# Four tiles for each buffer of gathered rows, and their four TensorE transposes placed at four points of a step

## The chip, the cores and the metric

The kernel runs on one core of one Trainium2 chip. The metric is device time in microseconds (us), from the start to the end of one execution. Names used here: TensorE (PE in the profile; PEld is its weight load, PEq and PEldq its sequencer), VectorE (DVE), ScalarE (ACT), GpSimd (POOL), and SyncE (SP), which only issues DMAs here. PSUM is the memory that TensorE writes, in banks of 128 x 512 float32.

## The reference

A graph of 12,500 nodes with 16 features and 412,500 directed edges, sorted by destination, goes through two blocks; each is followed by a residual and a normalisation over the 16 features. The first is a two-layer graph convolution. The second is a mesh network with two message-passing rounds, and it holds the change:

```
n = ln(mlp(x));  e = ln(mlp(edge_attr))                      # 64 features each
for s in range(2):
    ce  = concat([e, n[src], n[dst]])                        # one row of 192 per edge
    e   = e + ln(silu(ce @ w0[s] + b0[s]) @ w1[s] + b1[s])
    agg = segment_sum(e, dst)
    n   = n + ln(mlp(concat([n, agg])))
out = mlp(n)
```

`n[src]` is a gather of 412,500 rows at random places. `n[dst]` and the sum over `dst` are local, since the edges are sorted by destination.

## The kernel before

**Groups and steps.** Edges are taken in 405 groups of 1024: K = 8 columns of 128 edges, a column to a set of 128 partitions. `edge_step(s)` (L997) handles round s. Its `steps()` (L1048) is one long unrolled program: step g starts some stages of new groups and ends others of older groups, so that several groups are in flight. In round 0, step g computes the hidden layer of the edge encoder of group g (`hidden_enc`, L963), its second layer one step later, the block's hidden layer of group g - 3 (`hidden_blk`, L970), the block's second layer of group g - 4 and the segment sum of group g - 5. In round 1 there is no encoder, and the three block stages are 0, 1 and 2 steps behind. The call `tc.manual_schedule` (L1129) keeps TensorE, VectorE and ScalarE in exactly the order in which the program is written. SyncE and GpSimd are queues of their own, each in its own order, and they run ahead as far as their waits let them.

**The gathered rows.** The product of w0 with the sender's features is made once per node and stored in a table of [12500, 64] float32 in DRAM. `ahead(g)` (L1028) calls `gather` (L404), which issues eight indirect DMAs from GpSimd: each fetches 128 rows of 256 bytes into column k of a buffer `pg` of [128, 8, 64]. There are R = 5 such buffers in a ring, and `ahead` is called LA = 3 groups ahead. GpSimd does nothing else in these stages, and what holds it back is only that buffer g % 5 must have been read by the group five before. These waits are kept by pieces of the buffer: GpSimd's DMAs of columns 0, 2, 4 and 6 wait for one TensorE instruction each, the transposition of the pair of columns that they begin to overwrite.

**The block's hidden layer.** `hidden_blk` fills one PSUM bank. It multiplies w0's part for the edge features with `e` (float32, L974), adds the receiver's part by three bfloat16 products `qd` x `ot` (also L974; `qd` is a window of the receivers' table, `ot` a one-hot matrix), and then adds the gathered rows by four transposes against the identity (L976), one for each pair of columns. ScalarE reads the bank (SiLU, L979) into `h`, which the second layer (`second`, L984 for the bias and L986 for the products) takes in the next step.

**The order on TensorE in a step of round 0:** second layers of encoder and block (2 x L984, L986), transposes of normalised rows (`turned`, L994), segment sum (`window_sum`, L389, 8 columns x 2 operands), encoder's hidden layer (L965), then `hidden_blk`: `e` (L974), `qd` (L974), four transposes of `pg` (L976). Round 1 is the same without the encoder's parts and without L994. ScalarE's `h` (L979) ends every step, and the next step's second layer of the block begins with it. VectorE adds the segment sum of the step before at L397, builds `ot` at L1045 and the one-hot matrix of the sum at L377, and normalises (L466 to L471).

Of the kernel before, what the change touches and what calls it, by code (L numbers as in the profile page):

```python
# [9 lines left out]
F32 = mybir.dt.float32  # L10
# [8 lines left out]
P = 128  # L19
K = 8  # L20
W = 64
D = 64
GB = 135
SI, DR = 81, 45
R, LA = 5, 3
# [12 lines left out]
def gcn_then_mesh_gnn_kernel(ctx: ExitStack, tc: tile.TileContext, a: dict, out: bass.AP):  # L38
# [21 lines left out]
    nc = tc.nc  # L60
# [64 lines left out]
    def bank(name):  # L125
        return psum.tile([128, 512], F32, name=f"ps_{name}")
# [251 lines left out]
                                drl[:, g * K:(g + 1) * K, None].to_broadcast([P, K, W]), op=OP.is_equal)  # L378
        return oh

    def window_sum(oh, offs, g, val, acc, r0, m, later=None):


        ps = bank("seg")
        for k in range(K):
            r = r0
            for v in val(k):
                n = v.shape[1]
                nc.tensor.matmul(ps[r:r + n, :W], v, oh[:, k, :], start=(k == 0), stop=(k == K - 1))  # L389
                r += n  # L390

        def add():
            at = nc.values_load(offs[0:1, g:g + 1], engines=[ET.DVE], min_val=0, max_val=N,
                                skip_runtime_bounds_check_because="a destination is a node's number or N, and "
                                "the windows behind it are held to N")
            w = acc[r0:r0 + m, ds(at, W)]
            nc.vector.tensor_add(w, w, ps[r0:r0 + m, :W])  # L397

        if later is None:
            add()  # L400
        else:
            later.append(add)

    def gather(table, idx, to):  # L404

        for k in range(K):
            nc.gpsimd.indirect_dma_start(  # L407
                out=to[:, k, :], out_offset=None, in_=table,
                in_offset=bass.IndirectOffsetOnAxis(ap=idx[:, k:k + 1], axis=0))

    def trip_count(i, most):
        return nc.values_load(trips[0:1, i:i + 1], min_val=0, max_val=most,
# [554 lines left out]
        nc.scalar.activation(h, ph, AF.Silu, bias=ee_b0)  # L967
        return h

    def hidden_blk(s, e, pg, more=()):  # L970

        ph = bank("h")
        for i, (w, v) in enumerate([(eb_w0[s], e), *more]):
            nc.tensor.matmul(ph, w, v, start=(i == 0), stop=False)  # L974
        for j in range(KP):
            nc.tensor.matmul(ph[:, j * P:(j + 1) * P], pg[:, 2 * j:2 * j + 2, :].rearrange("p k f -> p (k f)"),  # L976
                             ident, start=False, stop=(j == KP - 1), is_transpose=True)
        h = work.tile([128, KP * P], F32, name="h")
        nc.scalar.activation(h, ph, AF.Silu, bias=eb_b0[s])  # L979
        return h  # L980

    def second(h, w1, b1):
        po = bank("o")
# [13 lines left out]
    def edge_step(s):  # L997


        ring = [work.tile([P, K, D], F32, name=f"pg{i}", bufs=1) for i in range(R)]  # L1000
        acc = (s01, 0, 128) if s == 0 else (ns2, D, D)

        ENC, ENC2, TURN, BLK, BLK2, SUM = (0, 1, 2, 3, 4, 5) if s == 0 else (None, None, None, 0, 1, 2)
# [23 lines left out]

        def ahead(g):  # L1028
            at = g % SI * K
            gather(tabs_p[s], srcs[g // SI][:, at:at + K], ring[g % R])  # L1030

        def send_window(g):
            at = nc.values_load(base_row[0:1, g:g + 1], engines=[ET.SP], min_val=0, max_val=N,
# [14 lines left out]
        def steps():  # L1048
            for g in range(2):
                send(g)  # L1050
                send_window(g)
            hot(0)
            later = []
            for g in range(NG + SUM + 1 + CHUNK):
                if real(g + 2):
                    send(g + 2)
                if g + 8 - SUM >= 0 and real(g + 8 - SUM) and (g + 8 - SUM) % DR == 0:
                    send_places((g + 8 - SUM) // DR)
                if real(g - BLK + LA) and g >= BLK:
                    if (g - BLK + LA + 8) % SI == 0 and real(g - BLK + LA + 8):  # L1060
                        send_sources((g - BLK + LA + 8) // SI)
                    ahead(g - BLK + LA)
                if real(g - BLK + 2) and g - BLK >= 0:
                    send_window(g - BLK + 2)

                while later:
                    later.pop(0)()

                if real(g - SUM + 1):
                    c = g - SUM + 1  # L1070
                    ohs[c] = one_hot(work, drls[c // DR], c % DR)
                if real(g - BLK + 1) and g - BLK >= 0:
                    hot(g - BLK + 1)

                parts = []
                if s == 0 and real(g - ENC2):
                    c = g - ENC2
                    y0[c] = work.tile([P, K, D], F32, name="y0", bufs=5)
                    parts.append((second(hids.pop(c), *ee1), y0[c]))
                if real(g - BLK2):  # L1080
                    c = g - BLK2
                    y1[c] = work.tile([P, K, D], F32, name="y")
                    parts.append((second(hidb.pop(c), *eb1[s]), y1[c]))
                if g - 1 in chunk_at:
                    c = chunk_at[g - 1]
                    ny[c] = work.tile([P, CB, D], F32, name="ny", bufs=1)
                    parts.append((node_second(nh, *nb1[s], n=P, name="seg"), ny[c]))
                if parts:
                    normalised(work, P, *parts)
                if s == 0 and real(g - TURN):  # L1090
                    c = g - TURN
                    es[c] = work.tile([128, KP * P], F32, name="e", bufs=6)
                    nc.scalar.activation(es[c], turned(y0[c]), AF.Identity, scale=e_g[0])
                if real(g - SUM):
                    c = g - SUM
                    y, e = [y1.pop(c)], es.pop(c)
                    if s == 0:
                        later.append(lambda c=c, e=e, pt=turned(y[0]): (
                            nc.vector.scalar_tensor_tensor(e, pt, e_g[1], e, op0=OP.mult, op1=OP.add),
                            nc.sync.dma_start(e1_d[:, col(c)], e)))  # L1100
                        y.insert(0, y0.pop(c))
                    window_sum(ohs.pop(c), base_row, c, lambda k: [v[:, k, :] for v in y], *acc, later)
                if s == 0 and real(g):
                    hids[g] = hidden_enc(feats.pop(g))
                if real(g - BLK):
                    c = g - BLK
                    hidb[c] = hidden_blk(s, es[c], ring[c % R], hots.pop(c))

                if g in chunk_at:
                    node_hidden(step_products(s, chunk_at[g]), nb_b0[s], nh)  # L1110
                if g - 2 in chunk_at:
                    c = chunk_at[g - 2]
                    step_update(s, c, node_turned(ny.pop(c)))
                if g - 3 in chunk_at:
                    c = chunk_at[g - 3]
                    if s == 0:
                        send_tables(1, c)
                    else:
                        dh[c] = decode_hidden(c)
                if s and g - 4 in chunk_at:  # L1120
                    c = chunk_at[g - 4]
                    decode_second(c, dh.pop(c))
# [113 lines left out]
```

## Time and profile before

The median is 16592.26 us, of 14 runs from 16435.23 to 18125.43 us. The profiled execution took 16677.06 us; its span from the first to the last instruction is 16675.1 us, and the mean clock granted to TensorE is 0.799 of the full one.

| stretch | from, us | length, us | steps |
|---|---|---|---|
| before round 0 (sort, convolution, tables) | 0 | 5466 | |
| round 0, steps with gathers | 5466.42 | 6210.30 | 400 |
| round 0, last steps, no gathers left | 11676.72 | 27.56 | 4 |
| between the rounds, start of round 1 | 11704.28 | 125.88 | |
| round 1, steps with gathers | 11830.16 | 4759.55 | 398 |
| round 1, last steps, no gathers left | 16589.71 | 22.30 | 4 |
| end | 16612.01 | 63 | |

Steps are counted from one ScalarE `h` (L979) to the next.

How lines are read. A line of waits gives the engine, the line that waited, what released it, the total in us, the number of times and the longest. "remote" means that the instruction began when a semaphore came in, and that the work which the trace names for it had ended well before. A line of the timeline gives start, length, engine, line, operation, tiles, and in brackets how long the engine had been idle and what ended that. A line of windows gives from:to, the length, then for each engine its busy us and its number of instructions, the granted clock of TensorE as a share, the DMA engines' share, and GB/s. The ends of matmuls are modelled, so their starts are used. SPq lines are DMAs that SyncE issues.

### The profile page before, as it was taken

To read this page: it belongs to the slowest core of one execution; us is meant where nothing else is said; L and a number is where in the kernel's file an instruction comes from. 1 tells how busy PE (TensorE), PEld (TensorE's weight loads), DVE (VectorE), ACT (ScalarE), POOL (GpSimd) and SP (SyncE) were. 2 spreads that over 40 slices of the span, in tenths; PEclk is the share of its full clock that TensorE was granted. 3 is DMA by queue.
4 is the path that set the end of the run, shared out by engine and by line. 5 is a ranking of instruction groups with operands and counts; after the bars stand their busy time and mean duration, and the time that the engine had idled before them with its cause. 6 is when DMAs were issued, how large, how long until landed. Compare 5 with 4: busy or idle time off the path is not lost. (4 is left out here: it accounts for less than half of the span.)

```text
span 16675.1 us, 273242 instructions
## 1 busy us (share of the span) xinstructions
PE 11848.1 (71%) x103832; PEld 8743.1 (52%) x104442; DVE 8838.4 (53%) x22535; ACT 2342.7 (14%) x3705; POOL 6211.7 (37%) x6598
## 2 busy tenths in 40 slices
PE   0096999899995777777777777777556666666665
PEld 0086999699993444444444444444344444444443
DVE  9976777577774444444444444444333433443434
ACT  3300000000001122222222222222111111111111
POOL 0000000000000554444544445444566666666665
PEclk9998999799995777777777777777777777777777
DMA  0002111111111222222222222222222222222222
GB/s 26 4 11 57 67 66 66 44 68 66 66 59 33 48 54 52 51 50 50 53 49 53 47 50 52 49 48 51 58 60 61 60 61 61 60 61 60 60 60 49
DMA packets 1009226, 873.88 MB, mean 52 GB/s; under 512 B 650006, under 2 KB 757370, under 8 KB 1007214
## 3 DMA queue, kind: packets, MB, share of 16 engines
q1 hardware_dynamic: 800512, 643.03, 13.3%
q0 software_dynamic: 207360, 212.75, 7.5%
q8 instruction: 855, 14.01, 0.3%
q14 instruction: 499, 4.09, 0.1%
HBM read 720.51 MB, written 134.51 MB: 51 GB/s over the span
## 5 line engine op out<-in xcount | busy, mean ns | idle before, releaser
L407 POOL DMA_INDIRECT pg<-tab_p,si x6480 | 6206.5, 958 | 9558.6 <-DMA qd<-tab_q 4585.0
L466 DVE TENSOR_REDUCE var<-sq 128x8 f32<-128x512 f32 (+2 forms) x1290 | 861.8, 669 | 3306.9 <-ACT sq L465 1791.5
L986 PE MATMUL ps_o<-eb_w,h 128*128 128x128 f32 x6480 | 1303.5, 363 | 1691.3 <-ACT h L979 1413.8
L598 PE MATMUL ps_h<-t,roh 128*128 128x112 bf16 (+1 forms) x39936 | 2132.0, 211 | 237.0 <-DVE roh L574 237.0
L389 PE MATMUL ps_seg<-oh,y 128*64 128x64 f32 x19440 | 1505.1, 256 | 937.0 <-issue 910.8
L598 PEld LDWEIGHTS <-roh 128*128 128x128 bf16 x39936 | 2011.0, 98 | 286.6 <-DVE roh L574 240.7
L986 PEld LDWEIGHTS ps_o<-eb_w,h 128*128 128x128 f32 x6480 | 1106.4, 258 | 1931.8 <-ACT h L979 1527.2
L389 PEld LDWEIGHTS ps_seg<-oh,y 128*64 128x64 f32 x19440 | 1240.5, 166 | 1099.5 <-issue 1072.0
L614 PE MATMUL ps_seg<-ohd,msg 128*112 128x112 f32 (+1 forms) x13312 | 1619.6, 266 | 0.0
L974 PE MATMUL ps_h<-e,eb_w 128*128 128x512 f32 x1620 | 1391.3, 945 | 130.0 <-issue 99.4
L614 PEld LDWEIGHTS ps_seg<-ohd,msg 128*112 128x112 f32 (+1 forms) x13312 | 1408.6, 173 | 0.5
L605 DVE TENSOR_TENSOR msg<-ps_h,wm 128x448 f32<-128x448 f32 (+1 forms) x1536 | 973.9, 634 | 459.9 <-PE ps_h L598 454.6
L602 DVE TENSOR_TENSOR ohd<-ior,rdrel 128x448 f32<-128x448 f32 (+1 forms) x1536 | 1009.9, 658 | 236.6 <-PE ps_seg L614 236.6
L465 ACT ACTIVATE sq<-ps_o 128x512 f32<-128x512 f32 (+1 forms) x1240 | 735.5, 593 | 2623.0 <-issue 910.4
L979 ACT ACTIVATE h<-ps_h,eb_b 128x512 f32<-128x512 f32 x810 | 556.1, 686 | 3625.2 <-remote 2382.2
L965 PE MATMUL ps_h<-at,ee_w 16*128 16x512 f32 x810 | 685.2, 909 | 327.2 <-issue 310.0
L974 PE MATMUL ps_h<-ot,qd 128*128 128x512 bf16 x1821 | 718.1, 491 | 194.8 <-issue 179.5
L974 PEld LDWEIGHTS <-qd 128*128 128x128 bf16 x2430 | 304.9, 126 | 1048.5 <-issue 995.6
L471 DVE TENSOR_TENSOR y<-ps_o,rs_y 128x512 f32<-128x512 f32 x1215 | 802.0, 688 | 86.3 <-issue 2.3
L377 DVE TENSOR_TENSOR oh<-iow,drl 128x512 f32<-128x512 f32 x1215 | 829.6, 683 | 12.4 <-DMA drl<-rel_d 5.3
L1045 DVE TENSOR_SCALAR ot<-rb,iop 128x512 bf16<-128x512 bf16 x810 | 283.9, 351 | 866.6 <-PE ps_h L974 761.5
L976 PEld LDWEIGHTS ps_h<-ident,pg 128*128 128x128 f32 x3240 | 534.4, 178 | 382.8 <-issue 292.9
(264 smaller groups left out, 11473.7 us busy)
## 6 DMA issues: line engine op xcount, KB each, us to landing
mod<-mod_d SPq DMA_DIRECT2D x256, 832.0 KB
rb<-relg_d SPq DMA_DIRECT2D x1620, 64.0 KB
pg<-tab_p,si POOLq DMA_INDIRECT x6480
e_d<-e SPq DMA_DIRECT2D x405, 256.0 KB
e<-e_d SPq DMA_DIRECT2D x405, 256.0 KB
qd<-tab_q SPq DMA_DIRECT2D x1620, 24.0 KB
at<-in_attrT SPq DMA_DIRECT2D x405, 32.0 KB
tab_q<-tabs SPq DMA_DIRECT2D x50, 187.5 KB
```

Of the source, the lines that this page charges most:

```text
L377: nc.vector.tensor_tensor(oh, iow[:, None, :].to_broadcast([P, K, W]), drl[:, g * K:(g + 1) * K, None].to_broadcast([P, K, W]), op=OP.is_e ...
L389: nc.tensor.matmul(ps[r:r + n, :W], v, oh[:, k, :], start=(k == 0), stop=(k == K - 1))
L407: nc.gpsimd.indirect_dma_start(out=to[:, k, :], out_offset=None, in_=table, in_offset=bass.IndirectOffsetOnAxis(ap=idx[:, k:k + 1], axis=0))
L465: nc.scalar.activation(sq, o.rearrange("p (k f) -> p k f", f=D), AF.Square, scale=D ** -0.5)
L466: nc.vector.tensor_reduce(v[:, i:i + k], sq, axis=AX.X, op=OP.add)
L471: nc.vector.tensor_tensor(y, o, r[:, i:i + k, None].to_broadcast(list(y.shape)), op=OP.mult)
L598: nc.tensor.matmul(pg[:, (j - j0) * sb * F:(j - j0 + 1) * sb * F], ohs[h][:, u, at * P:(at + 1) * P], t3[:, i, u, b:b + sb * F], start=(i ...
L602: nc.vector.tensor_tensor(ohd[:, :n, :], ior[:, None, :].to_broadcast([P, n, LR]), drel[:, j0:j0 + n, r:r + 1].to_broadcast([P, n, LR]), o ...
L605: nc.vector.tensor_tensor(msg[:, :n * sb * F].rearrange("p (j s f) -> p j s f", s=sb, f=F), pg[:, :n * sb * F].rearrange("p (j s f) -> p j ...
L614: nc.tensor.matmul(acc[:sb * F, :LR], msg[:, j * sb * F:(j + 1) * sb * F], ohd[:, j, :], start=(j0 + j == packs[0][0]), stop=((j0, n, sb) ...
L974: nc.tensor.matmul(ph, w, v, start=(i == 0), stop=False)
L986: nc.tensor.matmul(po[:, j * 128:(j + 1) * 128], h[:, j * P:(j + 1) * P], w1, start=False, stop=(j == KP - 1))
```

## The change

Each of the five buffers becomes four tiles of [128, 2, 64], one for each pair of columns; `gather` fills them in the same order with the same eight DMAs. `hidden_blk`, as used in `edge_step`, is taken apart into `begin_blk` (the product with `e`), four calls of `send_pair` (one transposition each) and `end_blk` (the three `qd` products and the SiLU). The order on TensorE in a step of round 0 becomes: second layers; `e`; pair 0; transposes of normalised rows; pair 1; first half of the segment sum; pair 2; second half; encoder's hidden layer; pair 3; `qd`. In round 1: second layer; `e`; pairs 0 and 1; first half of the sum; pair 2; second half; pair 3; `qd`. The instructions of ScalarE and VectorE keep their order. GpSimd issues the same DMAs in the same order with waits on the same kinds of events, pair by pair as before. On SyncE a store or load of `e` (or a load of `rb`) moves by three places in some 90 places of the program, and nothing else changes.

```diff
+    def window_sum(oh, offs, g, val, acc, r0, m, later=None, halfway=None):
         ps = bank("seg")
         for k in range(K):
+            if halfway and k == K // 2:
+                halfway()
...
+    def gather(table, idx, *to):
+        k = 0
+        for t in to:
+            for i in range(t.shape[1]):
+                nc.gpsimd.indirect_dma_start(
+                    out=t[:, i, :], out_offset=None, in_=table,
+                    in_offset=bass.IndirectOffsetOnAxis(ap=idx[:, k:k + 1], axis=0))
+                k += 1
...
-    def hidden_blk(s, e, pg, more=()):
-
+    def begin_blk(s, e):
         ph = bank("h")
-        for i, (w, v) in enumerate([(eb_w0[s], e), *more]):
-            nc.tensor.matmul(ph, w, v, start=(i == 0), stop=False)
-        for j in range(KP):
-            nc.tensor.matmul(ph[:, j * P:(j + 1) * P], pg[:, 2 * j:2 * j + 2, :].rearrange("p k f -> p (k f)"),
-                             ident, start=False, stop=(j == KP - 1), is_transpose=True)
+        nc.tensor.matmul(ph, eb_w0[s], e, start=True, stop=False)
+        return ph
+
+    def send_pair(ph, j, pair, stop=False):
+        nc.tensor.matmul(ph[:, j * P:(j + 1) * P], pair.rearrange("p k f -> p (k f)"), ident,
+                         start=False, stop=stop, is_transpose=True)
+
+    def end_blk(s, ph, more=()):
+        for i, (w, v) in enumerate(more):
+            nc.tensor.matmul(ph, w, v, start=False, stop=(i == len(more) - 1))
         h = work.tile([128, KP * P], F32, name="h")
         nc.scalar.activation(h, ph, AF.Silu, bias=eb_b0[s])
         return h
...
-        ring = [work.tile([P, K, D], F32, name=f"pg{i}", bufs=1) for i in range(R)]
+        ring = [[work.tile([P, 2, D], F32, name=f"pg{i}_{j}", bufs=1) for j in range(KP)] for i in range(R)]
...
+                b = g - BLK
+                pairs, ph = (iter(range(KP)) if real(b) else iter(())), None
+
+                def pair():
+                    for j in pairs:
+                        send_pair(ph, j, ring[b % R][j])
+                        break
...
+                if real(b):
+                    ph = begin_blk(s, es[b])
+                pair()
                 if parts:
                     normalised(work, P, *parts)
...
-                    window_sum(ohs.pop(c), base_row, c, lambda k: [v[:, k, :] for v in y], *acc, later)
+                    pair()
+                    window_sum(ohs.pop(c), base_row, c, lambda k: [v[:, k, :] for v in y], *acc, later, pair)
                 if s == 0 and real(g):
                     hids[g] = hidden_enc(feats.pop(g))
-                if real(g - BLK):
-                    c = g - BLK
-                    hidb[c] = hidden_blk(s, es[c], ring[c % R], hots.pop(c))
+                if real(b):
+                    for _ in range(KP):
+                        pair()
+                    hidb[b] = end_blk(s, ph, hots.pop(b))
```

More of the change, by code (lines that the diff above doesn't have):

```diff
@@ L379, in one_hot @@
         return oh
-    def window_sum(oh, offs, g, val, acc, r0, m, later=None):
+    def window_sum(oh, offs, g, val, acc, r0, m, later=None, halfway=None):
         ps = bank("seg")
         for k in range(K):
+            if halfway and k == K // 2:
+                halfway()
             r = r0
@@ L402, in window_sum @@
             later.append(add)
[L404 to L409, printed above, removed]
+    def gather(table, idx, *to):
[6 more added lines that the diff above has]
+                k += 1
     def trip_count(i, most):
@@ L980, in hidden_blk @@
         return h
+    def hidden_blk(s, e, pg):
+        ph = begin_blk(s, e)
+        for j in range(KP):
+            send_pair(ph, j, pg[:, 2 * j:2 * j + 2, :], stop=(j == KP - 1))
+        return end_blk(s, ph)
     def second(h, w1, b1):
@@ L1029, in ahead @@
             at = g % SI * K
-            gather(tabs_p[s], srcs[g // SI][:, at:at + K], ring[g % R])
+            gather(tabs_p[s], srcs[g // SI][:, at:at + K], *ring[g % R])
         def send_window(g):
```

## The prediction

> **What bounds the kernel now.** I read the page's slices first, then the waits, a table of stretches, and the timelines of single steps. The edge rounds take 11.1 of 16.7 ms, and only they hold changed code.
>
> The waits, and the groups' row for the transposes:
>
> ```profile
> POOL pg L407 <- PE ps_h L976: 2388.5, 426, 13.0
> ACT h L979 <- remote: 2382.2, 290, 26.0
> ACT h L967 <- PE ps_h L965: 1623.4, 267, 13.8
> ...
> L976 PE MATMUL ps_h<-ident,pg 128*128 128x128 f32 x3240 | 646.3, 331 | 100.8 <-issue 75.6 <-DMA pg<-tab_p,si 24.6
> ```
>
> TensorE hardly waits for gathered rows (24.6 us in all). GpSimd waits for TensorE's transposes, and ScalarE waits for TensorE; "remote" says that TensorE's recorded work was long over by then. What is late is shown by stretches: round 0 with gathers, its last steps without any, the same for round 1.
>
> ```profile
> 5466.42:11676.72 6210.30, 4740.69 (x27813) 2860.04 (x28212) 2743.85 (x8217) 1326.21 (x2074) 3047.28 (x3200) 0.75 0.22 51
> 11676.72:11704.28 27.56, 26.21 (x245) 18.59 (x248) 20.21 (x70) 8.76 (x15) 0.00 (x0) 0.97 0.12 41
> 11830.16:16589.71 4759.55, 2889.81 (x14051) 1986.14 (x14252) 1906.03 (x6888) 541.48 (x869) 3067.47 (x3184) 0.73 0.27 60
> 16589.71:16612.01 22.30, 19.89 (x134) 13.98 (x136) 15.75 (x61) 5.14 (x8) 0.00 (x0) 0.92 0.19 11
> ```
>
> A step of round 0 takes 6210.30/400 = 15.53 us, one of round 1 4759.55/398 = 11.96 us. When GpSimd has no gathers left, the same kind of step takes 8.82 us (ScalarE's `h` at 11676.72 and 11685.54; the encoder's parts still run) and 5.21 us:
>
> ```profile
> 11676.72 0.69 ACT L979 ACTIVATE h<-ps_h,eb_b 128x512 f32<-128x512 f32 x1 [3.45 <-PE ps_h L976]
> 11685.54 0.69 ACT L979 ACTIVATE h<-ps_h,eb_b 128x512 f32<-128x512 f32 x1 [1.45 <-PE ps_h L976]
> ```
>
> So gathers in flight cost TensorE 6 to 7 us a step, though it doesn't wait for them. How, one step of round 1 shows:
>
> ```profile
> 14011.13 0.69 ACT L979 ACTIVATE h<-ps_h,eb_b 128x512 f32<-128x512 f32 x1 [8.51 <-remote]
> 14011.20 0.98 POOL L407 DMA_INDIRECT pg<-tab_p,si  x1 [2.25 <-remote]
> ...
> 14017.78 0.60 PE L976 MATMUL ps_h<-ident,pg 128*128 128x128 f32 x4
> ...
> 14019.99 0.94 POOL L407 DMA_INDIRECT pg<-tab_p,si  x1 [0.30 <-issue]
> ...
> 14023.02 0.69 ACT L979 ACTIVATE h<-ps_h,eb_b 128x512 f32<-128x512 f32 x1 [8.45 <-remote]
> 14023.10 0.95 POOL L407 DMA_INDIRECT pg<-tab_p,si  x1 [2.17 <-remote]
> ```
>
> The transposes are over at 14018.4, but nobody hears of it before 14023.0: 3.0 us after the last of eight gathers began. TensorE's completions are held while GpSimd's gathers run on, and come out some 2.1 us after the last gather's end; GpSimd and ScalarE then start at once. The step is eight gathers and one pause: 8 x 1.25 + 1.9 = 11.9 us. In round 0:
>
> ```profile
> 8565.56 0.95 POOL L407 DMA_INDIRECT pg<-tab_p,si  x1 [4.66 <-PE ps_h L976]
> 8565.89 0.69 ACT L979 ACTIVATE h<-ps_h,eb_b 128x512 f32<-128x512 f32 x1 [2.27 <-PE ps_h L976]
> ...
> 8571.51 0.28 PE L389 MATMUL ps_seg<-oh,y 128*64 128x64 f32 x2 [0.96 <-issue]
> ...
> 8574.31 0.94 POOL L407 DMA_INDIRECT pg<-tab_p,si  x1 [0.30 <-issue]
> ...
> 8577.57 0.69 ACT L967 ACTIVATE h<-ps_h,ee_b 128x512 f32<-128x512 f32 x1 [7.75 <-remote]
> ...
> 8579.34 0.60 PE L976 MATMUL ps_h<-ident,pg 128*128 128x128 f32 x4
> 8579.88 0.95 POOL L407 DMA_INDIRECT pg<-tab_p,si  x1 [4.63 <-PE ps_h L976]
> 8580.04 0.69 ACT L979 ACTIVATE h<-ps_h,eb_b 128x512 f32<-128x512 f32 x1 [1.78 <-PE ps_h L976]
> ```
>
> The first 4 us or so after GpSimd's restart are free. Then TensorE itself stalls (the last products of the segment sum and the encoder's two products follow singly), until all is released at 8577.5, 3.2 us after the last gather began. Only now come `e`, `qd` and the transposes, while GpSimd stands idle until the first transposition: 4.6 us here, 2292.3 us in 395 waits or 5.8 us a step over round 0. A step is 11.5 us of gathers and release, and 4.0 us in which GpSimd waits.
>
> **The change part by part.** The sum is made against the profiled execution (16677.06 us), 0.5% above the median of the runs; I put the difference on the median.
>
> Four tiles for one: 8 DMAs a group at 0.95 us as before, and TensorE already waited pair by pair: 0. SyncE's moved DMAs (some 90 of its rows, three places, 0.3 to 0.6 us each in the timelines): between 0 and 90 x 3 x 0.6 = 160 us were all bare; they are issued in the first 3 us after the release, two steps ahead of use, so 0.
>
> Pairs taken apart: no instruction is added. Four transposes in a row start 0.11 us apart (8579.34, 0.60 us for four with the end's latency); a change of shape on TensorE costs about 0.1 us more (L994's last start to L389's first, 8569.21 to 8569.41). Pair 2 inside the sum and pair 3 before `qd` make about two such changes more: 0.2 us a step. In round 1 this lies under the gathers; in round 0 half may. Bounds 0 and 810 x 0.3 = 240 us; I take 405 x 0.2 = 80 us.
>
> Round 0, GpSimd's idle time. Before, the first transposition comes behind the release and behind `e` and `qd`. After, pairs 0 and 1 stand about where the segment sum stood, and pair 2 in it, in the part that TensorE reaches before it stalls. At the release they are done, so GpSimd restarts there and not 4 us later: its pause falls from 5.8 to about 2.2 us (3.15 less the last gather's 0.95), and its own cycle to 8 x 1.25 + 2.2 = 12.2 us. Late next is TensorE: behind the release it still has the rest of the sum (0.6), the encoder's product (0.9 to 1.7 by the clock), pair 3 and `qd` (0.8 to 1.4), 2.4 to 4.0 us with the hand-over, and the new gathers leave it some 3.6 to 4 us. What isn't out by then waits for the next release, 12.2 - 4 = 8 us later. ScalarE's SiLU of the block waits behind `qd` (now last on TensorE, and with it SyncE's loads of `qd` and `rb`); behind that SiLU wait the next second layers. With a share f of steps that miss, a step takes 12.2 + 8 f. The work to be done and the room for it nearly touch, so f is neither 0 nor a half; I take 0.2: 13.9 us, 1.63 us less, 405 x 1.63 = 660 us. Bounds: f = 0 gives -1350 us, f = 0.55 +430 us.
>
> Round 1: the release hands GpSimd four pairs before and after, since TensorE has done its whole step's work from its queue by then. `e` and pairs 0 and 1 move to about 4 us behind GpSimd's restart, at the edge of the free time, so they rarely get out early. Cycle 10.0 + 1.9 us as before: 0. Bounds: all pauses gone, 398 x 1.9 = 760 us less; a miss of 8 us in one step of ten, 320 us more.
>
> Sum: 80 - 660 = -580 us: 16677 - 580 = 16097 for a profiled execution, 16592 - 580 = 16010 for the median.
>
> The Trainium skill ("Perfetto Trace Analysis", Matmul Optimizations) says that matmuls should run back to back in batches, which speaks against taking four transposes apart, and its page "TensorE: Matmul & The Clock Gate" (Part 4) gives about 275 ns for one transposition in a kernel's context. By it four single ones cost 4 x (275 - 110) = 0.66 us a step, 535 us in 810 steps, and nearly all of the gain would go (an estimate from that page). The rows above show 0.1 us for a change of shape. The same page (Part 1) says that TensorE's clock halves after an idle window of about 3.4 us; the granted clock of 0.75 with gathers and 0.97 without agrees.
>
> **The rivals.**
> - *Both gains in full*: pairs out before every release, f near 0. For it: pairs 0 and 1 come early in TensorE's order. Against: the free 4 us are nearly used up. 12.2 us a step, -1350 us, 15240 us; some of round 1's pauses could go too.
> - *No change*: what matters is one pause per step, whoever is first. For it: TensorE's 24.6 us of waits for rows, and round 1's cycle of gathers and pause. Against: GpSimd's 5.8 us in round 0. With f = 0.4, or with the restart brought no nearer: 16510 to 16675 us.
> - *Slower*: gathers that start earlier run over the end of the step, which is free of them now (8577.5 to 8580.0), and hold back the completion of `qd`, on which the step ends. It decides at 12.2 + 8 f = 15.53, f = 0.42. For it: 33 to 36 us for the steps at the start of round 1, where GpSimd ran 26 gathers without a stop. Against: in most steps the work fits into the free time. At f = 0.6: 17.0 us a step, +595 us, 17190 us.
>
> **How the numbers follow.** Forecast 0.45 (f 0.1 to 0.37, 15,550 to 16,500), gains in full 0.18, no change 0.10, slower 0.27. Changes of 0.5% (83 us) are about what runs of this kernel can tell. Faster: 0.45 + 0.18 = 0.63. The range runs from the full gain of round 0 (15,250) to f = 0.52 (12.2 + 4.16 = 16.36, +0.83 x 405 = +336 us: 16,930); the forecast's own is 15,550 to 16,500.
>
> **What would show it.** GpSimd's wait for the transposes in round 0 falls from 5.8 to 2 to 3 us, and it restarts within 0.2 us of the release (ScalarE's encoder `h`, L967); steps of round 0 at 12 to 14 us with some of 18 to 20, of round 1 at 12; L979 waits for L974 now, 0.7 to 2 us behind L967; granted clock above 0.75. Wrong would be the forecast if round 0's steps stay at 15 to 16 us with GpSimd's waits moved to other pairs, if round 1 leaves 12 us, or if the hold lasts by the number of gathers outstanding, not by their running.

## The result and the profile after

The changed kernel is slower: 16,868.9 us (median of 10 runs, 16,853 to 16,925) against 16,585.3 us (47 runs) of the kernel before on the same chip, a ratio of 1.018 with a 95% interval of 1.016 to 1.021. The ratios here are of the fast runs alone, while the median of before takes in a few slow ones. The forecast was 16,010 us.

First the stretches that the prediction used, in the profiled execution of the changed kernel (span 16,873.3 us, 198 us longer): round 0 with gathers, its last four steps without, round 1 with gathers, its last four steps. Columns are from:to, length, busy us and instructions of PE, PEld, DVE, ACT and POOL, granted clock, DMA share, GB/s.

```profile
5469.01:11776.26 6307.25, 4477.08 (x27813) 2993.31 (x28212) 2717.10 (x8216) 1293.06 (x2074) 3134.84 (x3199) 0.74 0.21 50
11776.26:11803.88 27.62, 26.42 (x245) 18.06 (x248) 21.01 (x73) 9.08 (x15) 0.00 (x0) 1.00 0.12 41
11930.77:16790.64 4859.87, 2818.11 (x14051) 1786.68 (x14252) 1911.74 (x6887) 548.40 (x868) 3015.31 (x3183) 0.75 0.26 59
16790.64:16812.48 21.84, 19.65 (x135) 12.54 (x136) 16.61 (x64) 5.14 (x9) 0.00 (x0) 1.00 0.13 13
```

Round 0 lost 97 us (6307.25 - 6210.30; 15.77 us a step where there were 15.53), round 1 100 us (4859.87 - 4759.55; 12.21 for 11.96). All else is level. So neither the gain forecast for round 0 nor the nothing forecast for round 1 came.

The waits:

```profile
ACT h L973 <- remote: 2991.8, 390, 8.2
...
ACT h L991 <- remote: 2147.3, 306, 24.1
POOL pg L412 <- PE ps_h L983: 1993.1, 537, 8.6
...
POOL pg L412 <- remote: 1366.6, 730, 10.2
```

In the kernel before, the last of these lines was

```profile
POOL pg L407 <- remote: 714.4, 356, 11.4
```

Over the whole program, GpSimd's wait for a transposition that has just been made fell from 2388.5 to 1993.1 us, but its waits on work long done rose from 714.4 to 1366.6 us. In round 0 alone it now waits 4.4 us for a transposition (1731.4 us in 395 waits, before 2292.3 us in 395) and 1.75 us on work long done (679.8 us in 388 waits, before 26.4 us): about 6.0 us a step, where there were 5.8. And ScalarE's encoder `h` (L973), which before mostly followed its product, now waits 390 times, about once in every step of round 0, for a completion that is held back. One step of round 0 shows how the two go together (timeline: start, length, engine, line, operation, and in brackets the idle time before and what ended it):

```profile
8640.58 0.69 ACT L973 ACTIVATE h<-ps_h,ee_b 128x512 f32<-128x512 f32 x1 [7.86 <-remote]
...
8640.79 1.33 POOL L412 DMA_INDIRECT pg<-tab_p,si  x1 [1.77 <-remote]
8641.16 0.68 ACT L991 ACTIVATE h<-ps_h,eb_b 128x512 f32<-128x512 f32 x1
...
8641.32 2.08 PE L1004 MATMUL ps_o<-ee_w,h 128*128 128x128 f32 x8 [5.01 <-ACT h L973]
...
8642.42 0.95 POOL L412 DMA_INDIRECT pg<-tab_p,si  x1 [0.30 <-issue]
...
8645.73 1.91 PE L978 MATMUL ps_h<-e,eb_w 128*128 128x512 f32 x2
...
8647.43 0.42 PE L983 MATMUL ps_h<-ident,pg 128*128 128x128 f32 x1
...
8648.13 0.94 POOL L412 DMA_INDIRECT pg<-tab_p,si  x1 [4.76 <-PE ps_h L983]
...
8649.91 0.69 PE L392 MATMUL ps_seg<-oh,y 128*64 128x64 f32 x16
...
8650.52 1.12 PE L971 MATMUL ps_h<-at,ee_w 16*128 16x512 f32 x2
...
8651.57 0.33 PE L983 MATMUL ps_h<-ident,pg 128*128 128x128 f32 x1
...
8651.95 0.59 PE L989 MATMUL ps_h<-ot,qd 128*128 128x512 bf16 x2
...
8654.37 0.94 POOL L412 DMA_INDIRECT pg<-tab_p,si  x1 [0.30 <-issue]
8656.74 0.22 DVE L400 TENSOR_TENSOR s<-s,ps_seg 128x64 f32 x1 [4.88 <-remote]
...
8656.84 0.69 ACT L973 ACTIVATE h<-ps_h,ee_b 128x512 f32<-128x512 f32 x1 [7.56 <-remote]
...
8657.05 1.33 POOL L412 DMA_INDIRECT pg<-tab_p,si  x1 [1.74 <-remote]
8657.42 0.68 ACT L991 ACTIVATE h<-ps_h,eb_b 128x512 f32<-128x512 f32 x1
```

At the release (8640.58) GpSimd does restart within 0.2 us, as forecast, but it has only the two gathers of pair 3 to make. Then it idles 4.76 us for pair 0 of the next group, which on TensorE lies behind both second layers and `e` and comes 6.3 us after ScalarE's `h`. Pairs 0, 1 and 2 then let six gathers go in one run. TensorE finishes pair 3 and `qd` by about 8652.5, in the same run, and nobody hears of it until 8656.84, 2.5 us after the last of the six began. The segment sum (L392) and the encoder's product (L971) are held too: they end 2.5 and 3.5 us after the run of six began, and the engines that wait for them, VectorE (L400) and ScalarE (L973), start at the release. So each step has two runs of gathers, of six and of two, and two waits. Over round 0 there are 376 runs of each kind; from the start of a run's last gather to the next gather it takes a median of 2.71 us after six and 5.54 us after two, so the cycle is 5 x 1.25 + 2.71 + 1.25 + 5.5 = 15.7 us.

Why does pair 0 take 6.3 us? The same step in four stretches:

```profile
8641.16:8645.60 4.44, 4.28 (x17) 3.62 (x18) 1.09 (x3) 1.28 (x3) 1.90 (x2) 0.50 0.36 100
8645.60:8648.50 2.90, 2.90 (x10) 1.76 (x10) 1.70 (x7) 0.60 (x1) 0.37 (x1) 0.54 0.12 40
8648.50:8652.30 3.80, 3.75 (x44) 2.24 (x43) 3.04 (x10) 0.69 (x1) 2.88 (x4) 1.00 0.10 20
8652.30:8657.42 5.12, 0.57 (x3) 0.09 (x1) 0.69 (x2) 0.58 (x1) 2.77 (x4) 0.77 0.13 24
```

TensorE now has all its idle time in one piece, 5 us ahead of the release, and then has a granted clock of 0.50 and 0.54 for some 7 us: just for the second layers, `e` and pair 0, on which GpSimd waits.

### The profile page after: what moved, and what is told of

Its sections match the earlier page's. It is cut to its first block, busy times and chain, and to the rows that moved or that the text cites. A ratio compares the mean times of both kernels' runs of the same rounds, so it can differ in the third digit from the quotient of the medians.

```text
span 16873.3 us, 273577 instructions
## 1 busy us (share of the span) xinstructions
PE 11510.6 (68%) x103832; PEld 8672.6 (51%) x104442; DVE 8817.9 (52%) x22535; ACT 2316.4 (14%) x3705; POOL 6248.4 (37%) x6598
## 5 line engine op out<-in xcount | busy, mean ns | idle before, releaser
L1004 PE MATMUL ps_o<-eb_w,h 128*128 128x128 f32 x6480 | 1553.0, 415 | 2023.0 <-ACT h L991 1859.5
L1004 PEld LDWEIGHTS ps_o<-eb_w,h 128*128 128x128 f32 x6480 | 1336.6, 306 | 2325.8 <-ACT h L991 1959.6
L1004 PE MATMUL ps_o<-ee_w,h 128*128 128x128 f32 x3240 | 826.8, 436 | 1827.8 <-ACT h L973 1806.8
L1004 PEld LDWEIGHTS ps_o<-ee_w,h 128*128 128x128 f32 x3240 | 708.5, 322 | 1966.3 <-ACT h L973 1934.6
L978 PE MATMUL ps_h<-e,eb_w 128*128 128x512 f32 x1620 | 1315.0, 909 | 24.5 <-DMA e<-e_d 24.5
L392 PE MATMUL ps_seg<-oh,y 128*64 128x64 f32 x19440 | 1190.5, 236 | 10.7 <-issue 6.7
L392 PEld LDWEIGHTS ps_seg<-oh,y 128*64 128x64 f32 x19440 | 960.1, 144 | 289.9 <-issue 176.3
L983 PE MATMUL ps_h<-ident,pg 128*128 128x128 f32 x3240 | 999.1, 332 | 9.6 <-DMA pg<-tab_p,si 9.6
L400 DVE TENSOR_TENSOR s<-s,ps_seg 128x64 f32 x405 | 88.9, 220 | 1477.3 <-remote 1462.4
L377 DVE TENSOR_TENSOR oh<-iow,drl 128x512 f32<-128x512 f32 x1215 | 832.5, 685 | 12.7 <-DMA drl<-rel_d 5.5
```

Source lines behind the costliest of these rows:

```text
L377: nc.vector.tensor_tensor(oh, iow[:, None, :].to_broadcast([P, K, W]), drl[:, g * K:(g + 1) * K, None].to_broadcast([P, K, W]), op=OP.is_e ...
L978: nc.tensor.matmul(ph, eb_w0[s], e, start=True, stop=False)
L983: nc.tensor.matmul(ph[:, j * P:(j + 1) * P], pair.rearrange("p k f -> p (k f)"), ident, start=False, stop=stop, is_transpose=True)
L1004: nc.tensor.matmul(po[:, j * 128:(j + 1) * 128], h[:, j * P:(j + 1) * P], w1, start=False, stop=(j == KP - 1))
```

## The experiments

Three theories were set against each other. **Runs**: what counts is how the order on TensorE cuts GpSimd's gathers into runs; each run holds TensorE's completions, from about 4 us after its start by the expectations, until 2.3 to 3.2 us after its last gather's start, and a step is TensorE's own work plus the holds. **Interleaving**: only the transpositions taken apart cost something. That one fits the result remarkably well. In the last steps, without gathers, there is no hold, and a step of round 1 takes

```profile
16801.56 0.69 ACT L991 ACTIVATE h<-ps_h,eb_b 128x512 f32<-128x512 f32 x1 [2.92 <-PE ps_h L989]
...
16807.02 0.69 ACT L991 ACTIVATE h<-ps_h,eb_b 128x512 f32<-128x512 f32 x1 [2.93 <-PE ps_h L989]
```

5.46 us where it took 5.21 before, and 798 steps x 0.25 us are 200 us of the 198 lost. (In the last four steps of round 0, shown above, nothing of it is seen: 27.62 us for 27.56.) **Clock**: what makes the step long is TensorE's half clock after its idle time.

The time of the kernel before differs from group to group of runs: in the four groups it took 16,585, 15,834, 15,875 and 16,673 us. Each group ran on one chip, the last three on three different ones; which one the first had isn't known, and no chip is known to have had two groups. So what is put down to the chip below may belong to the group. Ratios are therefore taken within a group, and across groups the steps and runs of gathers are compared. The table has all runs; steps are means over those with gathers in round 0 (400 of them).

| kernel | us | ratio to before, 95% | round 0, us a step | ScalarE's `h` to the first transposition, median us | runs of gathers in round 0 |
|---|---|---|---|---|---|
| before (first group) | 16,585 | 1 | 15.53 | 14.9 | 8 (388) |
| changed | 16,869 | 1.018 (1.016 to 1.021) | 15.77 | 6.2 | 6 (376), 2 (376) |
| `tiles4` | 15,858 | 1.002 (1.000 to 1.004) | 13.62 | 11.6 | 8 (385) |
| `e_early` | 15,971 | 1.009 (1.006 to 1.012) | 13.90 | 12.7 | 8 (388) |
| `together` | 17,832 | 1.127 (1.123 to 1.131) | 17.15 | 5.1 | 8 (397) |
| `halves` | 15,569 | 0.984 (0.981 to 0.988) | 12.89 | 5.9 | 4 (779) |
| `after_again` | 16,819 | 1.060 (1.056 to 1.065) | 15.61 | 6.2 | 6 (379), 2 (381) |
| `j2_late` | 15,579 | 0.982 (0.978 to 0.986) | 12.90 | 6.0 | 4 (783) |
| `late3` | 15,946 | 1.005 (1.003 to 1.008) | 13.88 | 5.3 | 8 (266), 6 (128), 2 (127) |
| `warm` | 16,689 | 1.053 (1.048 to 1.057) | 15.21 | 5.0 | 6 (381), 2 (380) |
| `warm20` | 16,241 | 0.974 (0.971 to 0.977) | 13.99 | 3.1 | 6 (346), 2 (352) |
| `halves_warm` | 15,711 | 0.942 (0.940 to 0.945) | 13.07 | 3.4 | 4 (479), 8 (158) |
| `halves_mid` | 15,970 | 0.958 (0.955 to 0.961) | 13.74 | 3.6 | 4 (320), 8 (219) |
| `half_gathers` | 13,479 | one run, no ratio | 12.91 | 6.2 | 4 (399) |

`tiles4` to `halves` ran as one group, `after_again` to `warm` as the next, the rest as the last.

**The tiles alone.** Four tiles, and TensorE's order of before:

```diff
-                if real(b):
-                    ph = begin_blk(s, es[b])
-                pair()
...
-                    for _ in range(KP):
-                        pair()
-                    hidb[b] = end_blk(s, ph, hots.pop(b))
+                    ph = begin_blk(s, es[b])
+                    add_windows(ph, hots.pop(b))        # qd
+                    for j in range(KP):
+                        send_pair(ph, j, ring[b % R][j], stop=(j == KP - 1))
+                    hidb[b] = silu_blk(s, ph)
```

> The four tiles alone, with the order of before on TensorE. All theories: the waits are the same pair by pair, so this is the time of before, within 0.4% (16,520 to 16,660 us). If the tiles were the cause, it would be 1.8% slower, like the changed kernel.

1.002 (1.000 to 1.004): the tiles are nothing; what is left is the order, and SyncE's moved DMAs with it. On this chip the order of before makes 13.6 us a step and not 15.5.

**`e` alone moved.** `tiles4`, with `begin_blk` left behind the second layers:

```diff
+                if real(b):
+                    ph = begin_blk(s, es[b])
                 if parts:
                     normalised(work, P, *parts)
...
-                    ph = begin_blk(s, es[b])
                     add_windows(ph, hots.pop(b))
```

> The order of before with the product of e alone moved behind the second layers (four tiles kept, pairs together at the end). Theory of the prediction (what stands between the release and the first transposition is GpSimd's idle time): e's 1.0 to 1.9 us leave that stretch, round 0 gets 400 to 760 us shorter, 15,850 to 16,200 us. Theory of runs (TensorE gets on only outside a hold that lasts from about 4 us after a run of gathers starts to 2.4 to 3.2 us after its last gather starts; a step is TensorE's own work plus its holds): e goes into the free time and pushes as much of the segment sum into the hold, 16,450 to 16,700 us. Theory of interleaving (taking transposes apart costs TensorE 0.25 us a step and nothing else matters): 16,500 to 16,700 us.

0.9% slower than before. The prediction's view that shortening the stretch between release and transposition shortens the step would have had 2 to 4.5% less; it is refuted: from the encoder's `h` (L973) to the first transposition it is now a median of 0.5 us, where `tiles4` has 2.6, but GpSimd's waits for transpositions in round 0 are longer (1642.6 us for 1456.4). Runs and interleaving both expected about nothing, and the loss is a little more than either allowed.

**The pairs kept together.** Behind `e`, none taken apart:

```diff
-                pair()
+                for _ in range(KP):
+                    pair()
...
-                    pair()
-                    window_sum(ohs.pop(c), base_row, c, lambda k: [v[:, k, :] for v in y], *acc, later, pair)
+                    window_sum(ohs.pop(c), base_row, c, lambda k: [v[:, k, :] for v in y], *acc, later)
```

> The changed kernel with its four pairs kept together, behind the second layers and e. Theory of interleaving: no transposition is taken apart, so the time of before, 16,550 to 16,650 us. Theory of runs: GpSimd starts a run of eight at the first transposition, 4.5 to 6.5 us after ScalarE's h; the 4.5 us of turned rows, sum, encoder and qd behind it don't fit into the 4 us that are free, so h comes with the release, 11.5 us after the run's start: 16 to 18.5 us a step in round 0, 200 to 1,200 us more, 16,750 to 17,800 us; runs of 8 in round 0, not of 6 and 2.

12.7% slower, 17.15 us a step, runs of eight. Interleaving falls, for all that its sum fits: the order that takes no pair apart is by far the worst. The first transposition comes 5.1 us after `h`, earlier than in the changed kernel, so "as early as possible" falls with it. Round 1 loses too: 13.23 us a step, 11.82 in `tiles4`.

**Two halves.** The same, with two calls of `pair()` behind `e` in place of four; the other two fall to the end, before `qd`.

> Pairs 0 and 1 together behind the second layers and e, pairs 2 and 3 together before qd. Theory of runs: GpSimd's gathers of a step of round 0 fall into two runs of four with a release after each; each run holds TensorE for some 2.2 us (from 4 us after its start to 3.75 + 2.4) and not 4.7 (run of six) or 7.3 (run of eight), TensorE idles under 3 us and keeps its clock: 12.5 to 14 us a step in round 0, 600 to 1,200 us less, 15,400 to 16,000 us. Theory of interleaving: one cut and not three, 16,600 to 16,700 us. Theory of the prediction (first transposition as early as possible, no matter how the rest lies): like the changed kernel, 16,800 to 16,900 us.

Faster than before by 1.6%, 12.89 us a step, runs of four. One cycle:

```profile
8108.33 0.94 POOL L412 DMA_INDIRECT pg<-tab_p,si  x1 [0.30 <-issue]
8111.54 0.94 POOL L412 DMA_INDIRECT pg<-tab_p,si  x1 [2.27 <-PE ps_h L983]
...
8115.28 0.94 POOL L412 DMA_INDIRECT pg<-tab_p,si  x1 [0.30 <-issue]
...
8117.38 0.69 ACT L973 ACTIVATE h<-ps_h,ee_b 128x512 f32<-128x512 f32 x1 [4.79 <-remote]
8117.59 1.32 POOL L412 DMA_INDIRECT pg<-tab_p,si  x1 [1.36 <-remote]
```

The run of four starts at 8111.54 and the release comes 5.8 us later, 2.1 us after its last gather began; in the changed kernel it came 8.7 us after the start of a run of six. GpSimd's two waits are 2.27 and 1.36 us, where they were 4.76 and 1.74.

**The changed kernel beside others on another chip, and pair 2 or pairs 1 and 2 moved to the end.** `j2_late` takes out `halfway`'s argument; `late3` also the `pair()` ahead of the sum:

```diff
-                    window_sum(ohs.pop(c), base_row, c, lambda k: [v[:, k, :] for v in y], *acc, later, pair)
+                    window_sum(ohs.pop(c), base_row, c, lambda k: [v[:, k, :] for v in y], *acc, later)
```

> The changed kernel itself, unedited, beside the three others on this chip. On the chip of the first runs before took 16,585 us, on that of the second 15,834 us, with 15.5 and 13.6 us a step in round 0. Theory of runs: the changed kernel's step of round 0 is fixed by its runs of six and two (6.25 + 2.7 + 1.25 + 5.5 = 15.7 us) on any chip, so its time stays at 16,800 to 16,900 us whatever before takes here. Theory of interleaving (0.25 us more of TensorE a step): 1.5 to 2% above before on any chip.

The changed kernel takes 16,819 us here, within 0.3% of the first group, while before takes 4% less than there. The loss is 6% on this chip and 1.8% on the first one, because the changed kernel's time is the same on both and that of before is not.

> The changed kernel with pair 2 moved from the middle of the sum to pair 3, before qd. Theory of runs: it turns the runs of six and two into four and four: 12.5 to 13.5 us a step in round 0, 900 to 1,300 us less than the changed kernel. Theory of interleaving: one cut of three is gone, some 70 us less than the changed kernel.

One transposition moved by half a sum and the encoder's product, and 1,240 us go (16,819 to 15,579): runs of six and two become four and four. This settles it between runs and interleaving: it still takes two pairs apart. Round 1 gains from it too, 4,960 to 4,801 us from its first `h` to its last; 343 runs of eight there, where the changed kernel mixes runs of 2, 4, 8, 10 and 12.

> The changed kernel with pairs 1 and 2 moved to pair 3, before qd. Theory of runs: runs of two (at pair 0) and six; the hold now falls where TensorE has second layers and e to do and not where it has nothing: 11.7 to 13 us a step in round 0, at or below the four and four of pair 2 moved alone. If the number of early pairs were what helps (the prediction's view), this would be slower than the changed kernel, which has three early, and than that with two.

13.88 us, a miss. Pair 0 comes 5.3 us after `h`, often before GpSimd has ended the six gathers of the group before, a run that now reaches to about 5.6 us after `h`. The runs of six and two join into one of eight in 266 steps, with its long hold. So two and six are no stable cut.

**The clock.** Products with a tile of zeros behind `qd` in round 0, ten and twenty of them, add nothing to the result and fill TensorE's idle time:

```diff
+                    more = hots.pop(b)
+                    if s == 0:
+                        more = more + [(more[0][0], zeros)] * 20
-                    hidb[b] = end_blk(s, ph, hots.pop(b))
+                    hidb[b] = end_blk(s, ph, more)
```

> The changed kernel with ten more products behind qd in every step of round 0, of qd with a tile of zeros, so that TensorE doesn't idle for the 5 us ahead of the release. Theory of the clock (the granted clock is 0.50 for 4.4 us after the release and 0.54 for the next 2.9, since TensorE idled 5 us before; so the second layers, e and pair 0 take 6.3 us and not 4.2): pair 0 comes 4.2 to 5 us after ScalarE's h, 1.3 to 2 us less a step, 500 to 800 us less than the changed kernel. If the clock doesn't matter, or if the ten products don't get out in the hold: the same time as the changed kernel, or up to 4 us more a step.

130 us less than the changed kernel in its group, short of the 500 to 800 expected. The ten take only 2.2 us; 2.8 us of idle time stay, and pair 0 comes earlier in every other step alone (steps of 14.8 and 16.1 us in turn).

> The changed kernel with twenty products by zeros behind qd in round 0, where ten (2.2 us) left TensorE idle for 2.8 us and brought pair 0 forward to 5.0 us after ScalarE's h in every other step only (14.8 us, the others 16.1). Theory of the clock: TensorE idles under 1 us now, the second layers, e and pair 0 run at the full clock in every step, pair 0 comes 4.2 to 5.0 us after h, 13.6 to 14.8 us a step: 300 to 700 us less than with ten. Theory that the clock is a side effect: as with ten, or longer by the 2.2 us of ten more products (up to 900 us).

Twenty do it, though they lengthen TensorE's work by 4.3 us. A step of that kernel, TensorE's clock in the stretch behind `h`:

```profile
8293.77:8297.40 3.63, 3.63 (x24) 2.76 (x24) 1.20 (x3) 1.88 (x3) 1.55 (x2) 1.00 0.59 142
```

and GpSimd's first gather of pair 0 and of pair 3:

```profile
8297.53 0.94 POOL L412 DMA_INDIRECT pg<-tab_p,si  x1 [1.90 <-PE ps_h L983]
...
8306.50 1.33 POOL L412 DMA_INDIRECT pg<-tab_p,si  x1 [1.79 <-remote]
```

The clock is 1.00 where it was 0.50, pair 0 comes 3.1 us after `h` where it came 6.2, and GpSimd's wait for it is 1.90 us for 4.76. A step takes a mean of 13.99 us for 15.6 or 15.8. So of the changed kernel's step some 1.6 to 1.8 us are the half clock (the two kernels ran on different chips); the runs of six and two stay.

**Halves and clock, halves and an earlier pair 0.** Eight products by zeros added to the halves; and the halves with `e` and pairs 0 and 1 between the two second layers in round 0:

```diff
+                if s == 0 and real(b):
+                    ph = begin_blk(s, es[b])
+                    pair()
+                    pair()
                 if real(g - BLK2):
                     c = g - BLK2
                     y1[c] = work.tile([P, K, D], F32, name="y")
```

> Pairs 0 and 1 behind e, 2 and 3 before qd, with eight products by zeros (1.7 us) behind qd in round 0. With the halves alone TensorE idles 2.2 to 2.4 us before each h, runs at half clock behind it, and most steps take 13.4 us, those with pair 0 at 5.0 us after h 12.1. Theory of the clock: all steps at 12.1 to 12.5 us, 150 to 500 us below the halves alone, 15,050 to 15,420 us. If the clock doesn't matter: as the halves alone, 15,570.

> As the halves, but in round 0 with e and pairs 0 and 1 between the two second layers. Theory of runs: pair 0 comes some 4 us after h, before the second run of four is over (4.7 us after h), so that the two runs join into one of eight: one hold of 7.3 us, as in before; 12 to 17 us a step, by whether TensorE's work gets out, so no gain over the halves or a loss of up to 1,600 us. Theory of the prediction (earlier is better): 12 to 12.5 us a step, 200 to 350 us below the halves.

Neither is better than the halves in round 0: 13.07 and 13.74 us a step against 12.89. For the second this was expected; for the first it was a miss, by the same mechanism. With the clock up, pair 0 comes 3.4 us after `h`, before the second run of four is over; 158 pairs of runs join into runs of eight, and 43% of the steps take 14 us or more, where 1% of those of the halves do; 39% take less than 12 us, which doesn't make up for them. So the halves are kept apart by TensorE's slow clock: it makes pair 0 late enough.

**Half the gathers.** In the changed kernel, pairs 2 and 3 are fetched for the first five groups only:

```diff
-            gather(tabs_p[s], srcs[g // SI][:, at:at + K], *ring[g % R])
+            n = KP if g < R else 2
+            gather(tabs_p[s], srcs[g // SI][:, at:at + 2 * n], *ring[g % R][:n])
```

> The changed kernel, with the gathers of columns 4 to 7 left out for all groups but the first five (the transpositions then read old rows, so its output is not the reference's); TensorE's order and work are the same. Theory of runs: one run of four a step, at pair 0, released 3.75 + 2.4 us after its start; 10.5 us a step in round 0 if h gets out ahead of the hold, 13.6 if it comes with the release; 6 to 7 us a step in round 1. If TensorE's own work at the clock it gets set the step, with no hold: 15 to 16 us in round 0 as before. If gathers cost nothing but their issue: 8.2 and 5.5 us, as in the last steps without any.

```profile
8063.25 0.94 POOL L412 DMA_INDIRECT pg<-tab_p,si  x1 [8.82 <-PE ps_h L983]
...
8066.99 0.94 POOL L412 DMA_INDIRECT pg<-tab_p,si  x1 [0.30 <-issue]
```

and ScalarE's encoder `h` in the same step:

```profile
8069.18 0.69 ACT L973 ACTIVATE h<-ps_h,ee_b 128x512 f32<-128x512 f32 x1 [4.98 <-remote]
```

The typical step takes 13.4 to 13.5 us, against 13.6 computed; the mean is 12.9, that of the halves with twice the gathers. (Round 1 takes 6.59 us a step, where 6 to 7 was expected.) TensorE does the same work in the same order, ending it at about 8067.5, and is heard 2.2 us after the last gather of a run of four began, not of six. That the hold comes from the run of gathers, and ends with it in runs of four to eight, is shown by this and by the halves. What in the chip makes it is not.

## Why the prediction was wrong

**The step that failed** is "At the release they are done, so GpSimd restarts there and not 4 us later: its pause falls from 5.8 to about 2.2 us". Three things were wrong in it. (Its "4 us" is also more than the step shown there has: from the release at 8577.57 to GpSimd's restart at 8579.88 it is 2.3 us, and gathers and release take 12.0 us, not 11.5.)
- *The pairs that are done before the release are also taken before it.* GpSimd's waits go pair by pair, so pairs 0 to 2, transposed in the free time, let their six gathers run 0.7 us later. At the release only pair 3's two are due. That pause was priced rightly (1.74 us idle in the step shown, 2.2 forecast).
- *The wait came back two gathers later.* The prediction asked what would be late next and named TensorE's `qd`. It didn't ask what GpSimd would wait for after pair 3: pair 0 of the next group, behind both second layers and `e`. That is 4.76 us, as long as the wait that was to go (4.6 in the step it showed). The sum has to have a second pause: 15.7 us a step, not 12.2 + 8 f.
- *The clock.* The prediction saw 0.75 in the stretch of before, expected more than that and priced nothing. It is 0.74 over round 0, but no mean tells that it is 0.50 just on the path to pair 0. `warm20` puts this at 1.6 to 1.8 us a step, some 650 to 710 us of round 0. With it filled the step takes 13.99 us, close to the forecast's 13.9, by other terms: two pauses of about 1.8 us and more work.

**f.** The forecast had a share of 0.2 of the steps in which `qd` misses the free time, at 8 us each. It misses in about every step, so the share was wrong; and so was the price, since the run that holds it has six gathers and not eight, and most of the hold lies beside the gathers themselves. The room that new gathers were to leave TensorE, "some 3.6 to 4 us", was too large as well. In the changed kernel the encoder's product, which ends 3 to 3.5 us after the run's start, is heard over 1 us late in 393 of 395 steps, and the sum is held from 2 to 2.5 us on. (The forecast's arithmetic slips here: 12.2 + 8 x 0.2 is 13.8 and not 13.9. That is 40 us in all and decides nothing.)

**The rival that came true** is the slower one: "gathers that start earlier run over the end of the step ... and hold back the completion of `qd`, on which the step ends". The mechanism is the measured one, in nearly every step. Its price, 17.0 us a step at f = 0.6, was too high: it is 15.77 with runs of six and two. That `together`, with runs of eight, took 17.15 is no confirmation of that sum. The measured 16,869 us lies in the range, near its upper end.

**No change** held one true sentence, that one pause per step matters and not who is first, but the second pause adds to it. **Both gains in full**, 12.2 us a step, wasn't reached by any order here; the halves came to 12.89, and steps near 12.1 are met in the order of before too (11% of its steps of round 0 are at or below 12.5 us, 53% on the chip of `tiles4`).

**The terms at nothing or little.** Four tiles, 0: 1.002 measured. Pairs taken apart, 0.2 us a step: 0.25 in the last steps of round 1 (5.46 for 5.21 us). Round 1, 0 with bounds of -760 and +320: +100 us, inside the bounds; by `j2_late` it is the cut of pair 2 that breaks its runs of eight. That is half of the loss, and how the broken runs lengthen a step of round 1 was not followed further. SyncE's moved DMAs were not tried alone.

**The rules of the Trainium skill that were weighed.** "Matmuls back to back" (Perfetto Trace Analysis, Matmul Optimizations) speaks against the change, and the change lost; but with 0.25 us for three cuts, and with the four kept in one batch (`together`) 12.7% slower, the batches are not the reason. The clock rule (TensorE: Matmul & The Clock Gate, Part 1), quoted in the prediction as only agreeing, was the one to work out: after 5 us of idle time the clock here is 0.50.

**Where the better version lies.** The halves beat the kernel before where they ran, at 0.984 of it (0.981 to 0.988), and lie over 7% below the changed kernel of the other groups; `j2_late`, one argument taken out, does the same (0.982), 7.4% below the changed kernel of its own group. Why the kernel before takes 15.5 us a step on one chip and 13.6 on another, in the same order, stays open; its steps are a mixture of a cycle of 12.1 us and steps of 14 to 18, and the shares differ, with a granted clock over round 0 of 0.75 and 0.81.

## What to carry to other kernels

When a queue that is waited for is released piece by piece, follow each piece through a whole cycle of the loop and not to the next event alone: a wait that is removed at one piece can come back at the next, and a cycle can get a second pause. Read the clock in stretches within a step, since an idle time that is gathered into one piece is paid by whatever comes right behind it. And a sum that fits the result to 1% (0.25 us x 798) is no proof: one run of the opposite arrangement refuted it.

## What was unexpected of the hardware

- A run of indirect gathers holds TensorE's completions mainly by its own end, and somewhat by its length. From the start of the last gather to GpSimd's next start, where that is a "remote" one at the release, it takes a median of 2.3 to 2.8 us after runs of four, 2.6 to 2.7 after six, 2.9 to 3.2 after eight and 3.5 to 3.8 after twelve. It was foreseen for runs of eight only.
- The start of the hold is no fixed time after the run's start. In the changed kernel the sum is held 2 to 2.5 us after it. In a run of eight of `late3` that began at 8106.00, ScalarE still hears the second layer at 8112.32, 6.3 us on. And in the one long run, 56 gathers from 11749.14 to 11817.92 at the start of round 1 of the kernel before, a transposition made at 11770.60 is heard 23 us late, but in the middle of the run:

```profile
11770.60 0.41 PE L976 MATMUL ps_h<-ident,pg 128*128 128x128 f32 x1 [2.34 <-DMA pg<-tab_p,si]
```

```profile
11793.78 0.69 ACT L979 ACTIVATE h<-ps_h,eb_b 128x512 f32<-128x512 f32 x1 [25.97 <-remote]
```

So in that run it is a delay and not a stop until the run's end. What sets the start of the hold stays open.
- TensorE's clock was halved after less idle time than the expectations of these runs took. In the halves kernel TensorE idled 2.35 us and was then granted 0.51:

```profile
8118.12 2.07 PE L1004 MATMUL ps_o<-ee_w,h 128*128 128x128 f32 x8 [2.35 <-issue]
```

```profile
8117.97:8122.40 4.43, 4.28 (x17) 3.62 (x18) 1.08 (x3) 1.28 (x3) 3.52 (x4) 0.51 0.39 102
8122.40:8125.00 2.60, 2.60 (x8) 1.46 (x8) 1.43 (x6) 0.60 (x1) 0.33 (x2) 0.52 0.26 60
8125.00:8129.00 4.00, 4.00 (x48) 2.45 (x46) 3.30 (x11) 0.69 (x1) 3.09 (x4) 1.00 0.09 16
```

It stayed there for some 7 us of nearly full work before it came back to 1.00. In this trace the clock changes on a grid of 3.41 us: it is 1.00 from 8114.67 to 8118.08, a stretch in which TensorE is busy for 1.10 us, then 0.50 for two such stretches, from 8118.08 to 8124.91, and 1.00 after. So how the idle time lies to that grid may count beside its length; no run tried the two apart. The Trainium skill (TensorE: Matmul & The Clock Gate, Part 1) names an idle window, and a window of work, of about 3.4 us each; the measured 2.35 and 7 us decide here.
- Two kernels of the same operations differ in how much they vary from chip to chip, or group to group: the one before by 5% over four groups, and by 4% between the two in which the changed one differs by 0.3%.
